# Gathered rows as matmul weights: transposed sums, 32 targets per tile, and a set-up with fewer products

## The chip, the cores and the metric

The kernel runs on one core of a Trainium2 chip. A core has five engines with queues of their own: PE (TensorE, matrix products), DVE (VectorE), ACT (ScalarE), POOL (GpSimd, which here issues the indirect gathers) and SP (SyncE, which issues plain transfers). Sixteen DMA engines move the data. The metric is the time on the device in microseconds; the kernel before takes 1398.12 us, the median of three runs (1397.97 to 1398.96).

## The reference

Everything is float32. For B = 16 batches, N = 1024 nodes and D = 256 features, with `adj` a sparse weighted adjacency that serves as both A_a and A_m:

```python
pre_u  = einsum('bud,dk->buk', h, W1[:d])
pre_v  = einsum('bvd,dk->bvk', h, W1[d:])
hidden = relu(pre_u[:, :, None, :] + pre_v[:, None, :, :] + b1)
S   = sigmoid(einsum('buvk,ko->buvo', hidden, W2)[..., 0] + b2[0])
a_t = einsum('buv,bud->bvd', S * A_a, h)
m_t = einsum('uv,bud->bvd', A_m, h) * h
z   = beta1*h + beta2*(a_t @ Wa + ba) + beta3*(m_t @ Wm + bm)
```

Of the 1024 x 1024 pairs (u, v) 9052 have an edge. The kernels compute the gate only for these.

## The kernel before

**Tiles and loops.** The 1024 targets v are cut into 8 blocks of 128, each block into two windows of 64. The edges of a window are laid out one after another, sorted by target, in five tiles of 128 slots. The 16 batches are worked through in 4 groups of 4. So there are 32 block steps (`k`, group by group), ten tiles each, 320 tiles (`n`).

**Lists (`lists`).** For each block DVE finds up to 24 sources per target (line 173, three rounds of eight maxima), numbers their slots, and builds a 0/1 matrix that says which target owns which slot (`mark`). It goes to DRAM (`who`) and is loaded from there for each window (`load_mark`, line 420). Five matrix products with that matrix as weights (line 211) carry target data to slots. From them come the indices `uidx`, `vidx` and a one-hot row of 64 targets per slot. Then POOL gathers the edge values, ten small indirect transfers per list, all at once (line 237). Four lists (`EARLY`) are made ahead of the tiles, the others beside the first tiles, one step of the generator per tile.

**Rows (`rows`).** For each 128 nodes and each group, PE multiplies the transposed input hT with the two halves of W1 (line 291). The u half goes to a DRAM table, next to a copy of x (a row is 2048 numbers: 1024 of pre_u and 1024 of h). The v half gets b1 from DVE (`keep`, line 280) and stays in `pv`. In the set-up both halves are made for all eight blocks of group 0; those of the next group are made beside the tiles of the present one.

**Halves (`halves`).** For the block to come, `pv` is split in a rounded part and a remainder (lines 310 to 325), so that one pass in the format fp32r over both gives the full value. PE swaps the remainder to the other 64 partitions with a permutation (line 322).

**A tile.** `fetch` (line 411) gathers 128 table rows of 8 KB into one of five buffers. `expand` (line 427) spreads the targets' pre_v over the slots: mark as weights, two products of 512 columns. `gate` adds the two on DVE (line 441), takes ReLU times W2 with a sum (line 445, one instruction per batch), and ACT does the sigmoid (line 448). `left_adj` (line 435) makes one-hot times edge value, and line 450 multiplies it with the gate. `aggregate` (line 458) has these 128 columns, 64 targets without and 64 with the gate, as weights and the gathered h, 256 columns, as moving operand: four products per tile, whose sums of 128 partitions (two kinds of 64 targets) x 256 gather in `acc` over the five tiles.

**Window and block end.** ACT copies `acc` to `ev` (line 465), DVE multiplies the ungated half with h (line 469), PE transposes the whole (line 480) and ACT copies it to `LT` (lines 482, 483). `block_end` multiplies with Wm and Wa (line 498, `LT` as weights), and DVE adds beta1 h and the biases (lines 490, 504).

**Order.** Each engine does its instructions in the order of the program; that order is written by hand in the loop over `n` (a step per tile), and `after(step, f)` puts work off to a later step. At step n: aggregation of tile n-1, the fetch that its buffer allows, gate of tile n, put-off work, window and block ends, a step of the lists, pieces of the halves and rows, and the expansion of tile n+2. POOL's queue holds value gathers and row fetches in the order of issue.

Of the kernel before, what the change touches and what calls it, by code (L numbers as in the profile page):

```python
# [17 lines left out]
def kernel(  # L18
# [36 lines left out]

    nc = tc.nc
# [10 lines left out]
    S = 24  # L67
    RC = 5 + S
# [7 lines left out]
    who = [dram.tile([W, E], FP, name=f"who{w}") for w in range(NT * NW)]  # L76
# [42 lines left out]

    ahead = fixed([P, P], "ahead")  # L120
# [10 lines left out]
    slot, nth, place = upto, upto[:, :S], upto[:, :W]  # L131
# [4 lines left out]
    onehot = const.tile([P, NT * NW, TW, W], mybir.dt.bfloat16, name="onehot")  # L136
# [10 lines left out]
    pvp = main.enter_context(tc.tile_pool(name="pvp", bufs=NT))  # L147
# [13 lines left out]
    def lists(vt):  # L161
# [6 lines left out]
        unread = one.tile([P, N], mybir.dt.bfloat16, name="unread")  # L168
# [12 lines left out]
        nc.vector.scalar_tensor_tensor(R[:, 4:5], late, -float(W), row, ALU.mult, ALU.add)  # L181
# [8 lines left out]
        nc.vector.tensor_scalar(held, first, -1.0, float(E), ALU.mult, ALU.add)  # L190
        nc.vector.tensor_scalar(held, held, 0.0, R[:, 0:1], ALU.max, ALU.min)
        nc.vector.tensor_tensor(R[:, 0:1], R[:, 0:1], first, ALU.add)
        nc.vector.tensor_tensor(rest[:, vt:vt + 1], count, held, ALU.subtract)
        early = wk.tile([P, E], FP, name="early", bufs=1)
        nc.vector.tensor_scalar(early, slot, R[:, 0:1], None, ALU.is_lt)
# [3 lines left out]
        mark = big.tile([P, E], FP, name="made", bufs=2)  # L199
        nc.vector.scalar_tensor_tensor(mark, slot, first, early, ALU.is_ge, ALU.mult)  # L200
# [4 lines left out]
        RR = wk.tile([P, NW, RC], FP, name="RR", bufs=2)  # L205
        for w, mine in enumerate((soon, late)):
            nc.vector.tensor_scalar(RR[:, w, :], R, mine, None, ALU.mult)
            nc.sync.dma_start(who[vt * NW + w], mark[w * W:(w + 1) * W])
        pe = aside(vt)
        for j in range(TW):  # L210
# [6 lines left out]
                       pe[:, :M * RC].rearrange("p (j w r) -> p w j r", w=NW, r=RC))  # L217
        s_of = wk.tile([P, M], FP, name="s_of", bufs=2)
# [12 lines left out]
        yield  # L231
        nc.vector.tensor_tensor(onehot[:, sl].rearrange("p w j v -> p (w j) v"),
                                place.unsqueeze(1).to_broadcast([P, M, W]),
                                L[:, :, 4:5].to_broadcast([P, M, W]), ALU.is_equal)
        for i in range(vt * NW, (vt + 1) * NW):
            for j in range(TW):
                nc.gpsimd.indirect_dma_start(  # L237
                    out=val[:, i, j:j + 1], out_offset=None, in_=adj_flat,
                    in_offset=bass.IndirectOffsetOnAxis(ap=vidx[:, i, j:j + 1], axis=0),
                    bounds_check=N * N - 1, oob_is_err=False)  # L240
# [16 lines left out]
    pv, hTs = {}, {}  # L257

    def load_hT(k):
        g, nt = divmod(k, NT)  # L260
        if g < NG:
            hTs[k] = big.tile([P, GB, DC, P], FP, name="hT")
            nc.sync.dma_start(hTs[k].rearrange("p b c n -> p (b c) n"),
                              xT_rows[:, g * GB * DC:(g + 1) * GB * DC, nt * P:(nt + 1) * P])

    def rows(k):

        g, nt = divmod(k, NT)
        step = yield
        load_hT(k + 1)  # L270
        nc.scalar.dma_start(table[g][nt * P:(nt + 1) * P, GD:].rearrange("n (b d) -> n b d", b=GB),
                            x_rows[nt * P:(nt + 1) * P, g * GB:(g + 1) * GB, :])
        hT = hTs.pop(k)
        tab = big.tile([P, GD], FP, name="tab")

        def keep(c, p):
            if c.start == 0:
                pv[k] = pvp.tile([P, GD], FP, name="pv")
            m = (c.stop - c.start) // D
            nc.vector.tensor_tensor(pv[k][:, c].rearrange("p (b d) -> p b d", b=m),  # L280
                                    p.rearrange("p (b d) -> p b d", b=m),
                                    b1_b.unsqueeze(1).to_broadcast([P, m, D]), ALU.add)
        for wt in (w_u, w_v):
            for h in range(2):
                c = slice(2 * h * D, (2 * h + 2) * D)
                if wt is w_v and g == 0 and h == 0:
                    both = psa.tile([P, GD], FP, name="acc")
                p = both[:, c] if wt is w_v and g == 0 else small("p")
                for bb in range(2):
                    for i in range(DC):  # L290
                        nc.tensor.matmul(p[:, bb * D:(bb + 1) * D], hT[:, 2 * h + bb, i, :], wt[:, i, :],  # L291
                                         start=(i == 0), stop=(i == DC - 1))
                if wt is w_u:
                    nc.scalar.copy(tab[:, c], p)  # L294
                    if h == 1:
                        after(step + 1, lambda: nc.sync.dma_start(table[g][nt * P:(nt + 1) * P, :GD], tab))
                elif g:
                    after(step + 1, lambda c=c, p=p: keep(c, p))
                elif h == 1:
                    after(step + 1, lambda both=both: keep(slice(0, GD), both))  # L300
                if h == 0 or wt is w_u:
                    step = yield
# [218 lines left out]
    for n in range(NF):  # L521
        fetch(n)
# [160 lines left out]
```

## Time and profile before

| what | us |
|---|---|
| median of three runs | 1398.12 |
| profiled execution | 1396.24 |
| its span | 1394.4 |
| PE busy / PE weight loads busy | 1268.1 / 1076.6 |
| DVE busy | 1189.4 |
| ACT busy | 901.2 |
| POOL busy | 453.9 |

The busy times overlap. A PE share close to one means that matmul records follow one another without a gap; what a record costs is read from the distance between starts. The DMA queues moved 411.38 MB, 296.70 of them the gathers of POOL's queue.

### The profile page before, as it was taken

What the parts mean: (1) busy time and instruction counts of PE and PEld (TensorE: products, weight loads), DVE (VectorE), ACT (ScalarE), POOL (GpSimd) and SP (SyncE); (2) the same over time, 40 slices, a digit from 0 to 9 for tenths busy, and PEclk for the clock granted to TensorE, in tenths of its full rate; (3) what the DMA queues carried; (4) which work ended last, traced back from release to release, by engine and by line L of the source; (5) the groups of instructions that cost most, each with busy time, mean ns of one, the idle gap of its engine ahead of it and who ended that gap; (6) DMA issues with size and microseconds to landing.
All of it is one profiled execution on the core that took longest, in us unless ns stands there. A gap on an engine that the chain in (4) does not pass through costs nothing.

```text
span 1394.4 us, 20649 instructions
## 1 busy us (share of the span) xinstructions
PE 1268.1 (91%) x5920; PEld 1076.6 (77%) x5920; DVE 1189.4 (85%) x3424; ACT 901.2 (65%) x2554; POOL 453.9 (33%) x411
## 2 busy tenths in 40 slices
PE   6854888878999999999999999999999989999997
PEld 5743766667888888888888888888888777777775
DVE  8736898897888998888888998888888999999995
ACT  3113555555767777777776776767767777777763
POOL 2564245244322332222222322222222333333330
PEclk9976999989999999999999999999999999999999
DMA  6757856956999999999999899999998998999992
GB/s 190 225 170 280 274 197 229 328 182 229 339 354 313 312 363 334 310 323 346 334 331 314 308 349 333 315 313 331 331 343 302 322 322 307 310 310 317 314 320 76
DMA packets 152250, 411.38 MB, mean 295 GB/s; under 512 B 18128, under 2 KB 101584, under 8 KB 115920
## 3 DMA queue, kind: packets, MB, share of 16 engines
q0 software_dynamic: 48640, 296.70, 60.3%
q1 hardware_dynamic: 74112, 73.93, 16.2%
q10 hardware_dynamic: 29376, 39.33, 9.6%
q8 instruction: 50, 0.82, 0.2%
q14 instruction: 72, 0.59, 0.1%
HBM read 412.66 MB, written 52.95 MB: 334 GB/s over the span
## 4 chain that ended last, share of the span: by engine, by line
issue 32%; DVE 27%; DMA 13%; PE 12%; POOL 11%; ACT 3%; POOLq 1%; SPq 0%; DVEq 0%; ACTq 0%
POOL fetched L411 11%; DMA fetched<-table,uidx 10%; DVE t L445 10%; DVE t L441 9%; PE acc L458 4%; PE misc L291 3%; PE misc L498 2%; ACT left L450 1%; DVE ev L469 1%; DMA key<-in_adjT_dram 1%; DVE R L173 1%; DVE h_blk L490 1%; DMA val<-in_adjT_dram,vidx 1%; PE pc L427 1%; DMA hT<-in_xT_dram 1%
## 5 line engine op out<-in xcount | busy, mean ns | idle before, releaser
L458 PE MATMUL acc<-fetched,left 128*128 128x256 f32 x2560 | 618.0, 385 | 38.8 <-ACT ev L465 19.5
L411 POOL DMA_INDIRECT fetched<-table,uidx x320 | 350.6, 1096 | 839.6 <-PE acc L458 703.9
L458 PEld LDWEIGHTS acc<-fetched,left 128*128 128x128 f32 x2560 | 486.4, 192 | 134.5 <-ACT left L450 33.4
L445 DVE SCALAR_TENSOR_TENSOR t<-t,w_b 128x256 f32<-128x256 f32 x1280 | 470.0, 422 | 21.5
L441 DVE TENSOR_TENSOR t<-fetched,pc 128x1024 f32<-128x1024 f32 x320 | 388.7, 1215 | 96.3 <-DMA fetched<-table,uidx 62.2
L450 ACT ACTIVATE left<-left,gt 128x64 f32<-128x64 f32 x1280 | 340.9, 337 | 10.4
L427 PE MATMUL pc<-X,mark 128*128 128x512 f32 x640 | 244.1, 463 | 31.1 <-DVE t L441 28.0
L448 ACT ACTIVATE gt<-sc,b_b 128x4 f32<-128x4 f32 x320 | 95.8, 299 | 269.8 <-DVE t L445 268.1
L435 ACT ACTIVATE left<-onehot,val 128x256 f32<-128x256 bf16 x320 | 157.8, 493 | 2.1 <-DMA hT<-in_xT_dram 2.1
L427 PEld LDWEIGHTS pc<-X,mark 128*128 128x128 f32 x640 | 118.2, 192 | 47.4 <-DVE t L441 29.2
L498 PE MATMUL misc<-w_m,LT 128*128 128x256 f32 x512 | 135.1, 387 | 6.6 <-ACT LT L483 2.9
L291 PE MATMUL misc<-w_u,hT 128*128 128x256 f32 x512 | 125.1, 390 | 11.7 <-DMA hT<-in_xT_dram 8.7
L498 PE MATMUL misc<-w_a,LT 128*128 128x256 f32 x512 | 131.9, 380 | 0.0
L291 PEld LDWEIGHTS misc<-w_u,hT 128*128 128x128 f32 x512 | 98.2, 195 | 26.5 <-issue 8.7
L498 PEld LDWEIGHTS misc<-w_m,LT 128*128 128x128 f32 x512 | 96.2, 192 | 27.1 <-DVE h_blk L504 8.4
L237 POOL DMA_INDIRECT val<-in_adjT_dram,vidx x80 | 92.6, 1158 | 67.9 <-DVE eq L221 36.3
L294 ACT COPY tab<-misc 128x512 f32<-128x512 f32 x64 | 37.4, 584 | 116.8 <-PE misc L291 104.3
L498 PEld LDWEIGHTS misc<-w_a,LT 128*128 128x128 f32 x512 | 97.6, 191 | 13.3
L445 DVE DVE_READ_ACCUMULATOR t<-t,w_b 128x1 f32 x1280 | 104.2, 81 | 0.0
L325 ACT CAST X<-misc 64x512 fp32r<-64x512 f32 x128 | 74.2, 580 | 34.6 <-PE misc L322 32.7
L291 PE MATMUL misc<-w_v,hT 128*128 128x256 f32 x384 | 91.2, 380 | 2.0 <-ACT LT L483 1.7
L469 DVE TENSOR_TENSOR ev<-ev,h_blk 64x1024 f32<-64x1024 f32 x64 | 78.0, 1219 | 10.6 <-ACT ev L465 9.6
(90 smaller groups left out, 915.2 us busy)
## 6 DMA issues: line engine op xcount, KB each, us to landing
mark<-who ACTq DMA_DIRECT2D x128, 160.0 KB, 7.7
hT<-in_xT_dram SPq DMA_DIRECT2D x32, 512.0 KB, 10.3
table<-in_x_dram ACTq DMA_DIRECT2D x32, 512.0 KB, 8.8
table<-tab SPq DMA_DIRECT2D x32, 512.0 KB, 7.9
h_blk<-in_x_dram SPq DMA_DIRECT2D x32, 512.0 KB, 15.8
out_dram<-h_blk SPq DMA_DIRECT2D x32, 512.0 KB, 5.3
fetched<-table,uidx POOLq DMA_INDIRECT x320, 8.7
key<-in_adjT_dram SPq DMA_DIRECT2D x8, 512.0 KB, 8.1
```

The source lines that it names most:

```text
L237: nc.gpsimd.indirect_dma_start(out=val[:, i, j:j + 1], out_offset=None, in_=adj_flat, in_offset=bass.IndirectOffsetOnAxis(ap=vidx[:, i, j: ...
L291: nc.tensor.matmul(p[:, bb * D:(bb + 1) * D], hT[:, 2 * h + bb, i, :], wt[:, i, :], start=(i == 0), stop=(i == DC - 1))
L411: nc.gpsimd.indirect_dma_start(out=fetched[n % NF], out_offset=None, in_=table[g], in_offset=bass.IndirectOffsetOnAxis(ap=uidx[:, vt * NW ...
L427: nc.tensor.matmul(pcs[n][:, c], marks[n // TW][:, j * P:(j + 1) * P], cuts[k][:, w, c], start=True, stop=True)
L435: nc.scalar.activation(lefts[n][:, :, w, :], onehot[:, i, j, :].unsqueeze(1).to_broadcast([P, GB, W]), AF.Copy, scale=val[:, i, j:j + 1])
L441: nc.vector.tensor_tensor(t, fetched[n % NF][:, :GD].rearrange("p (b d) -> p b d", b=GB), pcs.pop(n).rearrange("p (b d) -> p b d", b=GB), ...
L445: nc.vector.scalar_tensor_tensor(t[:, b, :], t[:, b, :], 0.0, w2_b, ALU.max, ALU.mult, accum_out=sc[:, b:b + 1])
L448: nc.scalar.activation(gt, sc, AF.Sigmoid, bias=b2_b)
L450: nc.scalar.activation(lefts[n][:, b, 1 - w, :], lefts[n][:, b, w, :], AF.Copy, scale=gt[:, b:b + 1])
L458: nc.tensor.matmul(accs[n // TW][:, b, :], left[:, b].rearrange("p k v -> p (k v)"), f[:, GD + b * D:GD + (b + 1) * D], start=(j == 0 and ...
L469: nc.vector.tensor_tensor(ev[m0:m0 + W], ev[m0:m0 + W], hbs[k][m0:m0 + W], ALU.mult)
L498: nc.tensor.matmul(pz[:, bb * D:(bb + 1) * D], LTs[k][:, b * DC + c, i, :], wt[:, c, :], start=(i == 0 and c == 0), stop=(i == 1 and c == ...
```

## The change

- **Aggregation.** Per tile and batch there are now two products instead of one: a gathered block of 128 slots x 128 features is the weights, and 64 columns (32 targets without and with the gate) move. The sums come out with features on partitions and targets on columns. Tile j of a window holds only targets from `LO[j]` to `LO[j]` + 31, with `LO` = 0, 6, 20, 32, 32; an edge outside goes to the loop at the end of the kernel that handles what is left. The one-hot rows, `left` and the scaling by the gate have 32 columns instead of 64.
- **Window end.** Two ACT copies bring the sums to `LT`, ahead of the next gate; DVE multiplies with hT. Transposes, `ev` and the four copies are gone.
- **hT** stays in ten buffers for a group. Its load and the copy of x to the table are issued at one step of a block.
- **w_v and b1.** The v half is made in `halves`, one block ahead, for every block; b1 is added by a matrix product with an all-ones matrix and fp32r parts of b1 in two partitions (`spread`, `add_row`). So the set-up makes the u half only.
- **Block end.** The biases come in the same way, and h times beta1 is added in the instruction that reads the product.
- **Marks.** The 0/1 matrix is kept as bytes in SBUF for all windows (`whose`), written there by four SBUF transfers per list, and ACT casts it for each window.
- **Order.** `EARLY` is 3 instead of 4. Value gathers go to a list (`wanted`) and are issued two at a time next to the row fetches. One more step lies between the copy of `L` and its readers.

```diff
-    onehot = const.tile([P, NT * NW, TW, W], mybir.dt.bfloat16, name="onehot")
+    onehot = const.tile([P, NT * NW, TW, V], mybir.dt.bfloat16, name="onehot")
+    whose = const.tile([P, NT * NW, E], mybir.dt.uint8, name="whose")
...
+        few = wk.tile([P, E], mybir.dt.uint8, name="few", bufs=2)
+        nc.scalar.copy(few, mark)
         for w, mine in enumerate((soon, late)):
             nc.vector.tensor_scalar(RR[:, w, :], R, mine, None, ALU.mult)
-            nc.sync.dma_start(who[vt * NW + w], mark[w * W:(w + 1) * W])
+            for h in range(2):
+                nc.sync.dma_start(whose[h * W:(h + 1) * W, vt * NW + w, :], few[w * W:(w + 1) * W])
...
+        wanted.extend((i, j) for i in range(vt * NW, (vt + 1) * NW) for j in range(TW))
+    def fetch_val(n):
+        for i, j in wanted[:n]:
+            nc.gpsimd.indirect_dma_start(
+                out=val[:, i, j:j + 1], out_offset=None, in_=adj_flat,
+                in_offset=bass.IndirectOffsetOnAxis(ap=vidx[:, i, j:j + 1], axis=0),
+                bounds_check=N * N - 1, oob_is_err=False)
+        del wanted[:n]
...
+    def add_row(p, parts):
+        nc.tensor.matmul(p, unit, parts.unsqueeze(1).to_broadcast([P, 2, D]),
+                         start=True, stop=False, skip_group_check=True)
...
     def halves(k):
-        top = one.tile([P, GD], FR, name="top")
-        nc.scalar.copy(top, pv[k])
-        yield
         X = cuts[k] = big.tile([P, NW, GD], FR, name="X")
         low = one.tile([P, GD], FR, name="low")
...
+        for h in range(2):
+            step = yield
+            c = slice(2 * h * D, (2 * h + 2) * D)
+            p = small("p")
+            add_row(p, b1_p)
+            half_product(p, hTs[k], w_v, h, True)
+            nc.scalar.copy(X[:, 0, c], p)
+            after(step + 1, lambda c=c, p=p: nc.vector.tensor_tensor(
+                low[:, c], p, X[:, 0, c].bitcast(FP), ALU.subtract))
...
     def load_mark(q):
         marks[q] = big.tile([P, E], FR, name="mark")
-        src = who[q % (NT * NW)]
-        for h in range(2):
-            nc.scalar.dma_start(marks[q][h * W:(h + 1) * W].bitcast(FP), src)
+        nc.scalar.copy(marks[q], whose[:, q % (NT * NW), :])
...
         for b in range(GB):
-            nc.tensor.matmul(accs[n // TW][:, b, :], left[:, b].rearrange("p k v -> p (k v)"),
-                             f[:, GD + b * D:GD + (b + 1) * D],
-                             start=(j == 0 and b % 2 == 0), stop=(j == TW - 1), skip_group_check=True)
+            for c in range(DC):
+                d = GD + b * D + c * P
+                nc.tensor.matmul(acc[:, b, c, :, LO[j]:LO[j] + V], f[:, d:d + P], left[:, 0:b + 2:b + 1, :],
+                                 start=(j == 0 and b % 2 == 0 and c == 0), stop=(j == TW - 1),
+                                 skip_group_check=True)
...
     def window_end(q, step):
...
+        for h in range(2):
+            i = slice(h * GB * DC // 2, (h + 1) * GB * DC // 2)
+            nc.scalar.copy(LT[:, i, :, v], acc[:, h * GB // 2:(h + 1) * GB // 2].rearrange("p b c k v -> p (b c) k v"))
         def times_h():
+            nc.vector.tensor_tensor(LT[:, :, 0, v], LT[:, :, 0, v],
+                                    hTs[k].rearrange("p b c n -> p (b c) n")[:, :, v], ALU.mult)
...
         if 1 <= n <= total:
             aggregate(n - 1)
+            fetch_val(2)
             if n - 1 + NF < total:
                 fetch(n - 1 + NF)
+            if n % TW == 0:
+                window_end(n // TW - 1, n)
         if n < total:
             gate(n)
```

290 lines of the change are left out of this document (146 added, 144 removed).

## The prediction

> **What bounds the kernel now.** I first cut the span by the add that opens each tile's gate (line 441): the set-up up to tile 0, tiles 0 to 49, 50 to 239, 240 to 309, and the last ten with the tail; one row more takes tiles 10 to 39. Columns of the first view: stretch and its us, then busy us (and instructions) of PE, PE weight loads, DVE, ACT and POOL, granted PE clock, DMA share, GB/s. The second counts the adds.
>
> ```profile
> 0.00:117.70 117.70, 71.69 (x318) 59.87 (x318) 70.00 (x162) 23.32 (x38) 59.94 (x55) 0.87 0.62 186
> 117.70:367.00 249.30, 206.98 (x907) 168.57 (x908) 217.35 (x625) 141.06 (x397) 101.32 (x89) 0.94 0.75 260
> 159.70:320.90 161.20, 133.19 (x591) 107.61 (x592) 140.10 (x398) 88.10 (x247) 70.17 (x60) 0.96 0.72 247
> 367.00:1094.00 727.00, 722.30 (x3447) 625.95 (x3446) 641.45 (x1866) 525.58 (x1502) 203.25 (x191) 1.00 0.95 327
> 1094.00:1338.80 244.80, 224.39 (x1052) 187.07 (x1051) 225.48 (x673) 186.01 (x541) 81.24 (x70) 1.00 0.92 315
> 1338.80:1394.40 55.60, 42.75 (x201) 35.13 (x199) 35.12 (x101) 25.24 (x82) 8.13 (x7) 0.97 0.51 180
> ```
> ```profile
> 117.70:367.00 249.30, 60.73 (x50) 0.94 0.75 260
> 159.70:320.90 161.20, 36.43 (x30) 0.96 0.72 247
> 367.00:1094.00 727.00, 230.80 (x190) 1.00 0.95 327
> 1094.00:1338.80 244.80, 85.00 (x70) 1.00 0.92 315
> ```
>
> So there are five stages with different limits. **A**, the set-up, 117.7 us. **B**, 50 tiles while the remaining edge lists are built, 4.99 us each; DVE is the busiest (87%). **C**, 190 tiles at 3.83 us, 38.3 us per block of ten: PE is busy 722 of 727 us, and nothing else can set the pace. **D**, 70 tiles at 3.50 us, without row products: DVE and PE both 92%. **E**, 55.6 us.
>
> Then the timeline around the end of A:
>
> ```profile
> 81.97 0.33 SPq L296 DMA_DIRECT2D table<-tab  x1
> ...
> 84.89 1.12 POOL L237 DMA_INDIRECT val<-in_adjT_dram,vidx  x1 [7.81 <-DVE s_of L219]
> ...
> 88.22 1.22 DVE L280 TENSOR_TENSOR pv<-acc,b_b 128x1024 f32<-128x1024 f32 x1
> ...
> 110.29 0.99 POOL L237 DMA_INDIRECT val<-in_adjT_dram,vidx  x1 [0.30 <-issue]
> 111.58 1.00 POOL L411 DMA_INDIRECT fetched<-table,uidx  x1 [0.30 <-issue]
> ...
> 117.77 1.22 DVE L441 TENSOR_TENSOR t<-fetched,pc 128x1024 f32<-128x1024 f32 x1 [28.33 <-DMA fetched<-table,uidx]
> ```
> ```profile
> table<-tab SPq DMA_DIRECT2D x32, 512.0 KB, 7.9
> ```
>
> DVE is done at 89.4 and the table at 82.0 + 7.9 = 89.9, but POOL first works off twenty edge-value gathers, 1.3 us apart, from 84.9 to 111.3. Row fetches stand behind them, and DVE waits 28 us.
>
> **The change, stage by stage.**
>
> *A.* The gathers are now issued two at a time, ahead of row fetches, so POOL's queue no longer holds the first fetch; the table is late next, and with it DVE. DVE's busy 70.0 us lose the eight bias adds (1.22 each, 9.8) and one list of four. A list costs 140.10/30 - 641.45/190 = 1.29 us per tile over ten tiles, 12.9 us. Some 34 constant instructions come in, mostly tiny ones of the kind below, the rest up to a bias copy's size: 6 us, an estimate.
>
> ```profile
> L198 DVE TENSOR_SCALAR held<-held 128x1 f32<-128x1 f32 x8 | 1.2, 154 | 0.3
> ```
>
> 70.0 - 9.8 - 12.9 + 6 = 53 us busy. At the present 78% (70.0/89.4) DVE ends at 68. The last two row pieces, their write (7.9) and the way from first fetch to first gate (117.77 - 111.58 = 6.2) follow partly behind it; I put the fetch at 72 and the first gate at 78. Bounds: DVE without any wait, 53 + 1 + 6.2 = 60; three lists at the 20 us apiece that they now occupy, 8 + 62 + 7 for the start and the constants, then 7.9 and 6.2, 91. PE's work here falls by w_v's half of the products, so it is no bound. **-40** (-58 to -27).
>
> *B.* Five lists instead of four run here, with the same DVE. Its other work:
>
> ```profile
> L469 DVE TENSOR_TENSOR ev<-ev,h_blk 64x1024 f32<-64x1024 f32 x64 | 78.0, 1219 | 10.6 <-ACT ev L465 9.6
> ...
> L504 DVE TENSOR_TENSOR h_blk<-misc,h_blk 128x512 f32<-128x512 f32 x64 | 44.0, 687 | 12.8 <-PE misc L498 12.7
> L490 DVE SCALAR_TENSOR_TENSOR h_blk<-h_blk,be,bias 128x1024 f32<-128x1024 f32 x32 | 41.0, 1280 | 0.0
> L314 DVE TENSOR_TENSOR low<-pv,top 128x1024 fp32r<-128x1024 f32 x32 | 39.0, 1219 | 0.0
> ...
> L280 DVE TENSOR_TENSOR pv<-misc,b_b 128x512 f32<-128x512 f32 x48 | 33.1, 690 | 16.2 <-PE misc L291 15.8
> ```
>
> Per block the bias adds go (2 x 0.69), and so does the scaled bias (1.28). The product with h becomes two of 512 columns at 0.69 instead of two at 1.22 (-1.06); the remainder `low` becomes two of 0.69 for 1.22 (+0.16). That is -3.56 per block, -18 over five blocks, +12.9 for the fifth list: 212 us busy of the present 217.35. Of the 32 us idle, this wait makes up most (17.1 in 150 to 367 us):
>
> ```profile
> DVE s_of L219 <- ACT L L216: 17.1, 4, 5.3
> ```
>
> The added step between the copy of L and its reader lets a gate run in between; I count 13 of the 17 as gained: 212 + 19 = 231. **-18** (-27, idle of 10; -5, idle unchanged).
>
> *C.* PE alone counts.
>
> ```profile
> 701.59 1.03 PE L498 MATMUL misc<-w_a,LT 128*128 128x256 f32 x4
> 702.26 0.81 PE L427 MATMUL pc<-X,mark 128*128 128x512 f32 x2
> 702.91 1.89 PE L458 MATMUL acc<-fetched,left 128*128 128x256 f32 x8
> 704.64 0.59 PE L291 MATMUL misc<-w_u,hT 128*128 128x256 f32 x2
> ```
> ```profile
> 36.34 1.32 PE L211 MATMUL pc<-RR,made 128*128 128x58 f32 x10
> 37.50 1.95 PE L291 MATMUL misc<-w_u,hT 128*128 128x256 f32 x8
> 39.29 1.22 PE L211 MATMUL pc<-RR,made 128*128 128x58 f32 x10
> 40.34 0.87 PE L291 MATMUL misc<-w_u,hT 128*128 128x256 f32 x3
> ```
> ```profile
> 708.55 1.04 PE L480 MATMUL misc<-ident,ev 128*128 128x128 f32 x8
> ```
>
> Starts, not durations, give the price, as matmuls overlap. A written fp32 product is two records. Today's aggregation is eight records per tile, (704.64 - 702.91)/8 = 216 ns apart. The new one has twice the products, each with a gathered 128 x 128 block as weights and 64 moving columns: sixteen records. Nearest is line 211 with 58 columns: ten records take 1.16 and 1.05 us, 116 and 105 ns apart, mean 110.5. Four times fewer columns only halve the price, so something other than the stream, which I take for the weight load, sets it. Per tile 16 x 0.1105 = 1.77 us for 1.73; per block +0.4. Line 480's sixteen transposes per block go, the spacing being about 109 ns (1.04 us less one record of 0.275, over 7): -1.74. Four bias rows of 512 columns are added; the pair of line 427 lies between four 216 ns records from 701.59 (to 702.45) and 702.91, so one costs 0.23: +0.93. Sum -0.41 per block, over 19 blocks **-8**. With 105 ns it is -25. For the dear end I read the weight loads of such a ten, 1.30 us less one of 0.19 over 9, 123 ns: +30. A row at 58 columns is so near to 64 that I keep its mean.
>
> *D.* Group 3's w_v products, formerly made ahead, now come here. PE without stalls: aggregation 17.3, line 427 4.6, block end 6.9, transposes 1.7, swap 0.5, 31 us per block (224.39/7 = 32.1 busy). After: 31 - 0.41 + 16 x 0.216 = 34.1, against 35.0 per block today; DVE falls to 32.2 - 2.2 = 30. I take 34.6, PE-bound: **-3** (-9 to +13).
>
> *E.* The tail loses the transposes and their copies:
>
> ```profile
> 1376.22 1.01 ACT L465 COPY ev<-acc 128x1024 f32<-128x1024 f32 x1 [1.37 <-PE acc L458]
> ...
> 1379.94 1.13 PE L498 MATMUL misc<-w_m,LT 128*128 128x256 f32 x4 [0.30 <-ACT LT L483]
> ```
>
> From the copy to the first product is 3.7 us; two ACT copies (1.17) and one DVE product (0.69) make 1.9. With a little DVE work saved, **-3**.
>
> At nothing I cost what PE's 99% in C hides: a mark matrix is now cast by ACT instead of loaded by DMA, about 0.7 us per window by the 0.584 us of 512 columns below, while ACT is busy 525.58 of 727 and loses four transposition copies per window; its cover gone, it is 0.14 us a tile. The hT loads and table copies move to one fixed step of a block, on the same SP and ACT queues, with the row product six steps (23 us) behind them, and what a table copy finds late would be the first fetches of the next group, six steps on. On SP a list's byte writes wait for one more ACT cast, and behind them stand hT loads and table writes; in B these have those same 23 us, in A they are inside the bounds above.
>
> **Sum.** -40 - 18 - 8 - 3 - 3 = -72: span 1394.4 to 1322.4. The profiled execution took 1396.24 (1.84 more), the median 1398.12 (another 1.9): **1326**.
>
> **Rivals.**
>
> 1. *The set-up gives half.* The table's last row, not POOL, may already be nearly as late: hT loads, table copies and writes share the DMA engines (0.62 busy in A) and the list writes hold SP. First gate at 97: 1326 + 19 = **1345**. For: PE and DVE wait for each other in A; against: the table stood at 90 with one list more.
>
> 2. *The window copies delay the gates.* ACT now copies the sums before the gate's sigmoid, so at each window end it sits waiting for the aggregation's last product with the sigmoid queued behind; PE's next aggregation waits for that sigmoid's weights.
>
> ```profile
> L448 ACT ACTIVATE gt<-sc,b_b 128x4 f32<-128x4 f32 x320 | 95.8, 299 | 269.8 <-DVE t L445 268.1
> ...
> L450 ACT ACTIVATE left<-left,gt 128x64 f32<-128x64 f32 x1280 | 340.9, 337 | 10.4
> ...
> L294 ACT COPY tab<-misc 128x512 f32<-128x512 f32 x64 | 37.4, 584 | 116.8 <-PE misc L291 104.3
> ```
>
> The way is 2 x 0.584 + 0.30 + 0.34 = 1.8 us. Covering it on PE are eight records of a block's end or of w_v (1.73) and the next expansion (0.46), 2.2 us. Were the cover gone, 52 window ends in C and D cost 94 us: 1326 + 94 = **1420, slower**; it decides from 72/52 = 1.4 us each. Against: 0.4 us are to spare.
>
> 3. *Weight loads do not hide.* The mean load row says 192 ns:
>
> ```profile
> L458 PEld LDWEIGHTS acc<-fetched,left 128*128 128x128 f32 x2560 | 486.4, 192 | 134.5 <-ACT left L450 33.4
> ```
>
> At 192 ns per record a tile takes 3.07 us, 1.30 more than forecast: +351 over the 270 tiles from C on, and in B PE's 207 + 65 us would pass the 231 by 41: about **1720**. If only the stream's share (64/256 of 216 = 54 ns) is added to the 110, 164 ns, it is +0.85 per tile, 230 and 19 in B: **1575**. The gain is eaten at 72/270/16 = 17 ns more, 127 ns. Against: 512 columns in 230 ns and 256 in 216 leave no room for a bare load, and line 211's records hold their load already.
> The Trainium skill, "TensorE: Matmul & The Clock Gate", part 3, The mechanism, says that weight loads overlap running matmuls only where the row group differs; all here use all rows, so by it the time would be the 1575. The trace disagrees: the rows just named show loads hidden at full rows.
>
> 4. *PE gets cheaper than that*: 100 ns and below by way of the long run of equal records. Then C falls towards DVE's 641.45/19 - 3.56 = 30 us, but DMA (0.95 busy, less 5% for the marks) holds it near 36: 19 x 1.9 less, **1290**.
>
> 5. *A target's edges miss their 32-wide tile* and the slow loop at the end runs. Counting the reference's adjacency, the fullest window has 607 edges and no edge misses its tile; I leave it no chance.
>
> **Chances.** Forecast 0.66, rival 1 0.12, rival 2 0.08 (three parts in four past the point), rival 3 0.07, rival 4 0.07. What a measurement can tell from no change is 0.2%, 3 us. Faster: 0.66 + 0.12 + 0.07 and a little of rival 2, 0.85; same 0.02; slower 0.13. The forecast's own range lets A, B, C and D be off by half of their bounds, all to one side: 25 less, 40 more, 1301 to 1366. The range takes in rivals 1 and 4 and the near side of 2: **1288 to 1372**.
>
> **What would show it.** The first gate's add at 78 us, with no run of value gathers ahead of the first fetch; 50 tiles in 231 us; aggregations of sixteen records near 110 ns apart, 1.77 us a tile, with PE over 98% busy in C at 37.9 us per block; D at 34.6 with PE the busiest. I am wrong if those records lie 127 ns apart or more, if PE idles at window ends for ACT's copies, or if the first gate comes after 100 us.

## The result and the profile after

The changed kernel takes **1355.89 us** (median of four runs, 1353.14 to 1358.41) against 1398.05 for the kernel before on the same chip: a ratio of **0.9704**, interval 0.9677 to 0.9731. Forecast were 1326 us, range 1288 to 1372. Of 72 us only 42 came. One run of `once` (below), 1386.93 us, was in a slower state of the chip, and its time there is that of the other three.

The profiled execution took 1355.8 us, its span is 1353.9. Here is the changed kernel cut by the add that opens each gate (line 494 now), with the columns of the prediction's first view:

```profile
0.00:90.00 90.00, 50.25 (x197) 39.37 (x197) 53.34 (x158) 23.64 (x39) 17.69 (x18) 0.86 0.75 227
90.00:339.70 249.70, 224.45 (x1244) 199.65 (x1244) 216.81 (x659) 123.56 (x388) 128.27 (x120) 0.84 0.75 250
339.70:1056.40 716.70, 716.70 (x4763) 664.58 (x4763) 582.76 (x1827) 434.18 (x1430) 206.62 (x197) 1.00 0.89 313
1056.40:1296.10 239.70, 239.70 (x1640) 223.14 (x1640) 212.12 (x672) 153.53 (x512) 75.14 (x71) 1.00 0.85 304
1296.10:1353.90 57.80, 46.59 (x259) 40.90 (x258) 31.34 (x97) 18.45 (x68) 7.37 (x7) 0.81 0.45 160
```

| stage | before | forecast | after | change forecast / measured |
|---|---|---|---|---|
| A, set-up to first gate | 117.7 | 78 | 90.0 | -40 / -27.7 |
| B, tiles 0 to 49 | 249.3 | 231 | 249.7 | -18 / +0.4 |
| C, tiles 50 to 239 | 727.0 | 719 | 716.7 | -8 / -10.3 |
| D, tiles 240 to 309 | 244.8 | 242 | 239.7 | -3 / -5.1 |
| E, last ten and tail | 55.6 | 52.6 | 57.8 | -3 / +2.2 |

The stages that PE bounds came slightly better than forecast. A gave two thirds, B nothing, and E went the wrong way. In B DVE is as busy as before (216.81 of 217.35) and the granted PE clock has fallen from 0.94 to 0.84, in E from 0.97 to 0.81.

The end of A, from the timeline of the changed kernel (start, duration, engine, instruction, in brackets the idle time before it and its releaser):

```profile
67.82 1.32 PE L251 MATMUL pc<-RR,made 128*128 128x58 f32 x10 [1.16 <-DVE RR L246]
68.98 3.68 PE L319 MATMUL misc<-w_u,hT 128*128 128x256 f32 x16
...
70.37 3.26 SPq L336 DMA_DIRECT2D table<-tab  x2
...
71.85 0.49 DVE L272 TENSOR_TENSOR onehot<-place,L 128x320 bf16<-128x320 f32 x1
...
82.31 1.00 POOL L467 DMA_INDIRECT fetched<-table,uidx  x1 [34.24 <-DMA table<-in_x_dram]
...
90.04 1.22 DVE L494 TENSOR_TENSOR t<-fetched,pc 128x1024 f32<-128x1024 f32 x1 [17.70 <-DMA fetched<-table,uidx]
```

No run of value gathers stands ahead of the first fetch any more; POOL has been idle for 34 us when it comes, and the releaser is a transfer to the table. The last row pieces stand in PE's queue behind the third list's product, which PE waits 1.16 us for; the later of the two row writes starts at 70.37 + 3.26 - 0.33 = 73.3. It lands 8.0 us later, at 81.3, and the fetch comes 1.0 us behind that. (The releaser's row names a copy of x. This group's last copy was issued at 69.2 already; the one issued at 72.7, which lands in the same moment as the row write, fills the next group's table, which this fetch doesn't read.) DVE's lists end at 72.3. From there to the fetch it takes 10 us, and to the gate another 7.7.

What DVE waits for in B of the changed kernel (us in total, times, longest; 17.7 of the first row is the wait that ends A):

```profile
DVE t L494 <- DMA fetched<-table,uidx: 18.0, 2, 17.7
DVE t L494 <- PE pc L481: 9.8, 4, 4.7
DVE key L206 <- DMA key<-in_adjT_dram: 9.2, 3, 4.0
DVE low L352 <- ACT X L351: 4.4, 3, 2.2
...
DVE s_of L260 <- ACT L L256: 0.3, 1, 0.3
```

And the same view of the kernel before:

```profile
DVE s_of L219 <- ACT L L216: 17.1, 4, 5.3
DVE key L169 <- DMA key<-in_adjT_dram: 1.8, 1, 1.8
...
DVE t L441 <- PE pc L427: 1.3, 1, 1.3
```

The wait that the prediction meant to see shrink went from 17.1 to 0.3 us. Three others took its place: the load of the next list's adjacency rows (`key`, 1.8 to 9.2), the expansions (1.3 to 9.8) and the rounded part of pre_v (`low`, 4.4).

In C, a tile's aggregation and its neighbours in PE's queue:

```profile
702.85 0.81 PE L481 MATMUL pc<-X,mark 128*128 128x512 f32 x2
703.50 1.89 PE L513 MATMUL acc<-left,fetched 128*128 128x64 f32 x16
705.23 1.08 PE L548 MATMUL misc<-w_m,LT 128*128 128x256 f32 x4
```

Sixteen records take 705.23 - 703.50 = 1.73 us, 108 ns each; forecast were 110.5. Three stretches of B show one of two clocks (the ninth column):

```profile
113.20:140.40 27.20, 25.20 (x99) 22.99 (x99) 21.87 (x74) 13.18 (x43) 18.47 (x19) 0.50 0.82 264
140.50:174.50 34.00, 31.15 (x201) 27.74 (x199) 31.51 (x90) 17.05 (x57) 19.02 (x18) 1.00 0.74 242
174.60:191.60 17.00, 16.01 (x58) 14.44 (x59) 13.51 (x50) 7.29 (x21) 2.43 (x3) 0.50 0.82 255
```

At 0.50 PE's records are busy for 25.20 of 27.20 us, 93%, and it gets 99 of them done in 27 us instead of 201 in 34. What stands right before the first fall of the clock in B, and the later part of the stretch behind it:

```profile
109.60:113.00 3.40, 1.57 (x10) 1.00 (x9) 3.25 (x8) 0.00 (x0) 2.79 (x3) 1.00 1.00 285
119.80:136.90 17.10, 17.06 (x70) 16.22 (x71) 14.81 (x58) 8.76 (x28) 12.92 (x14) 0.50 0.76 232
```

PE was busy for 1.57 of the 3.40 us before the fall, mostly because it waited 1.78 us for DVE. The other eight falls in B and E, up to PE's last product, come behind 3.40 us with 1.03 to 2.69 us of PE work. So a fall follows PE's waiting. Once down, the clock stays at 0.50 for 17 us in which PE's records leave no gap.

### The profile page after: what moved, and what is told of

Its sections match the earlier page's. It is cut to its first block, busy times and chain, and to the rows that moved or that the text cites. A ratio compares the mean times of both kernels' runs of the same rounds, so it can differ in the third digit from the quotient of the medians.

```text
span 1353.9 us, 24556 instructions
## 1 busy us (share of the span) xinstructions
PE 1277.7 (94%) x8096; PEld 1167.6 (86%) x8096; DVE 1096.4 (81%) x3413; ACT 753.4 (56%) x2434; POOL 435.1 (32%) x411
## 4 chain that ended last, share of the span: by engine, by line
PE 66%; DVE 12%; issue 8%; DMA 7%; POOL 3%; ACT 2%; SPq 1%; ACTq 0%; POOLq 0%; DVEq 0%
PE acc L513 29%; PE misc L548 13%; PE misc L319 12%; PE pc L481 8%; DVE t L498 4%; DMA fetched<-table,uidx 4%; DVE t L494 3%; POOL fetched L467 2%; PE misc L323 2%; DMA key<-in_adjT_dram 2%; DVE R L210 1%; POOL val L282 1%; PE misc L360 1%; DMA table<-in_x_dram 1%; ACT LT L526 1%
## 5 line engine op out<-in xcount | busy, mean ns | idle before, releaser
L513 PEld LDWEIGHTS acc<-left,fetched 128*128 128x128 f32 x5120 | 637.0, 196 | 50.6 <-ACT left L503 23.8
L513 PE MATMUL acc<-left,fetched 128*128 128x64 f32 x5120 | 625.2, 277 | 15.4 <-ACT left L503 15.4
L467 POOL DMA_INDIRECT fetched<-table,uidx x320 | 339.8, 1062 | 827.2 <-PE acc L513 613.9
L503 ACT ACTIVATE left<-left,gt 128x32 f32<-128x32 f32 x1280 | 306.5, 310 | 10.4
L481 PE MATMUL pc<-X,mark 128*128 128x512 f32 x640 | 251.9, 475 | 19.6 <-DVE t L494 18.1
L526 ACT COPY LT<-acc 128x512 f32<-128x512 f32 x128 | 68.7, 589 | 216.5 <-PE acc L513 216.5
L319 PE MATMUL misc<-w_u,hT 128*128 128x256 f32 x512 | 136.5, 416 | 17.8 <-DMA hT<-in_xT_dram 9.5
L319 PE MATMUL misc<-w_v,hT 128*128 128x256 f32 x512 | 122.7, 383 | 0.0
L548 PEld LDWEIGHTS misc<-w_a,LT 128*128 128x128 f32 x512 | 100.5, 196 | 14.5
L319 PEld LDWEIGHTS misc<-w_v,hT 128*128 128x128 f32 x512 | 99.0, 193 | 13.1
L489 ACT ACTIVATE left<-onehot,val 128x32 f32<-128x32 bf16 x320 | 97.7, 305 | 0.0
## 6 DMA issues: line engine op xcount, KB each, us to landing
h_blk<-in_x_dram SPq DMA_DIRECT2D x32, 512.0 KB, 12.7
```

The lines of the kernel that those rows point to most:

```text
L467: nc.gpsimd.indirect_dma_start(out=fetched[n % NF], out_offset=None, in_=table[g], in_offset=bass.IndirectOffsetOnAxis(ap=uidx[:, vt * NW ...
L481: nc.tensor.matmul(pcs[n][:, c], marks[n // TW][:, j * P:(j + 1) * P], cuts[k][:, w, c], start=True, stop=True)
L489: nc.scalar.activation(lefts[n][:, 0, :], onehot[:, i, j, :], AF.Copy, scale=val[:, i, j:j + 1])
L503: nc.scalar.activation(lefts[n][:, 1 + b, :], lefts[n][:, 0, :], AF.Copy, scale=gt[:, b:b + 1])
L513: nc.tensor.matmul(acc[:, b, c, :, LO[j]:LO[j] + V], f[:, d:d + P], left[:, 0:b + 2:b + 1, :], start=(j == 0 and b % 2 == 0 and c == 0), s ...
L526: nc.scalar.copy(LT[:, i, :, v], acc[:, h * GB // 2:(h + 1) * GB // 2].rearrange("p b c k v -> p (b c) k v"))
```

## The experiments

The theory after the result had three parts: the late table holds A; the waits for `key` and PE's lower clock take back the gain of B; the clock takes E. The rivals: in B one of the two alone, or nothing but DVE's own work; and in C that the 64 columns have a price. Stages are those of the table above, each from the profiled execution of the kernel.

**v64: 128 columns instead of 64.** All 64 targets of a window stay in each tile, so the moving operand is twice as wide and the products as many.

```diff
-    V = 32
-    LO = [0, 6, 20, 32, 32]
+    V = 64
+    LO = [0, 0, 0, 0, 0]
```
The one-hot rows compare with `upto[:, :V]` in place of `place`, are bytes instead of bf16, and `RR` has one buffer instead of two, for space.

> Every tile again takes all 64 targets of its window, so each aggregation product moves 128 columns instead of 64 with the same weights. Clock theory (stage B and the tail lost time because 64-column products leave the array idle half of the time and the clock is granted at half speed): granted clock in B, tiles 0 to 49, from 0.84 to 0.92 or more, B from 250 us to 240, the tail stage E from 58 to 55; C (tiles 50 to 239) and D stay at 717 and 240 us within 5, because the spacing of the records, 110 ns, is set by the weight load. Feeding theory (B lost its gain to late keys and the fifth list, the low clock only follows from PE waiting): clock and B unchanged. Third view, columns set the price: spacing 140 ns or more and C longer by over 90 us. Total by the clock theory 1343, by the feeding theory 1356, by the third over 1440.

Measured: **1342.78 us**, ratio 0.9587 (0.9561 to 0.9613): faster than with 64 columns. From v64's windows (B, C, E, then the first fall of the clock in its B) and its PE timeline:

```profile
90.52:334.15 243.63, 211.41 (x1243) 187.65 (x1244) 218.49 (x659) 130.16 (x388) 129.15 (x120) 0.90 0.77 256
334.15:1050.24 716.09, 716.09 (x4759) 663.46 (x4757) 583.00 (x1827) 459.32 (x1427) 207.96 (x197) 1.00 0.89 314
...
1291.68:1343.77 52.09, 40.47 (x268) 36.18 (x266) 31.25 (x97) 20.69 (x72) 7.75 (x7) 0.95 0.50 183
...
110.00:113.40 3.40, 1.68 (x11) 1.08 (x9) 3.25 (x6) 0.00 (x0) 2.79 (x3) 1.00 0.94 280
113.40:120.20 6.80, 4.67 (x19) 3.92 (x18) 6.73 (x18) 2.99 (x10) 5.28 (x6) 0.50 0.82 297
```
```profile
701.89 1.95 PE L509 MATMUL acc<-left,fetched 128*128 128x128 f32 x16
703.60 0.48 PE L356 MATMUL misc<-low,swap 128*128 128x512 f32 x1
```

Sixteen records take 703.60 - 701.89 = 1.71 us at 128 columns, 107 ns each, and C is 716.1 against 716.7. The second 64 columns are free: something that every record has, not its columns, sets its price. E falls by 5.7 us, with the clock at 0.95 instead of 0.81. B falls by 6.1, which two profiles of one kernel can differ by as well (the run "again", below). The clock falls at the same place as before and behind the same kind of gap, but is back at 1.00 after 6.8 us, the longest time in v64's B, instead of 27.3: the columns show in how long it stays down.

**warm: more work for PE in B.** Four bias rows that the expansion then overwrites go ahead of each of the first 50 expansions, 200 records of 0.23 us, 46 us of PE.

```diff
+        if n < 50:
+            for h in range(4):
+                add_row(pcs[n][:, (h % 2) * 2 * D:(h % 2 + 1) * 2 * D], b1_p)
```

> In the first 50 tiles four throw-away one-pass products of 512 columns (0.23 us each, 46 us of PE work in all) are put ahead of each expansion, into the same accumulator, which the expansion then overwrites. Clock theory: granted clock in B 0.95 or more, and B no longer than 250 us, rather 240, in spite of the added work. Feeding theory: the clock may rise, but B gets longer, 255 to 270 us, since PE's 224 busy us of 250 get 46 more. C, D and E unchanged within 4 us.

Measured: 1346.75 us, ratio 0.9623 (0.9602 to 0.9644). B of warm, and two of its waits:

```profile
90.08:331.32 241.24, 235.05 (x1436) 211.22 (x1436) 217.47 (x660) 123.89 (x388) 128.73 (x120) 0.97 0.77 258
```
```profile
DVE t L497 <- PE pc L484: 9.6, 7, 3.6
...
DVE key L206 <- DMA key<-in_adjT_dram: 0.3, 1, 0.3
```

With 46 us more work on PE, B is 8.5 us shorter and the clock is 0.97. But the waits for expansions, which a faster clock should shorten, stay at 9.6 (the added rows stand right ahead of the expansions), and the waits for `key` are gone, for a reason that the run doesn't show. So it doesn't separate the two causes.

**keyahead: the adjacency rows of the next list are loaded a list earlier.**

```diff
-        key = big.tile([P, N], FP, name="key", bufs=2)
-        nc.sync.dma_start(key, adjT[vt * P:(vt + 1) * P, :])
+        if vt not in keys:
+            load_key(vt)
...
+        key = keys.pop(vt)
...
+        if EARLY <= vt < NT - 1:
+            load_key(vt + 1)
```

> The key rows of the next list are loaded half a list (some 20 us) before they are used, for the lists built beside the tiles. Feeding theory: DVE's waits for the key in B go from 9.2 us to under 1, B from 250 to 241 us, and the clock in B rises a little with it; total 1347. Clock theory: the waits go, but B loses only part of them, 245 us or more, and the clock stays under 0.88; total 1352.

Measured: 1343.76 us, ratio 0.9618 (0.9584 to 0.9652). B of keyahead, and its DVE waits:

```profile
90.32:326.71 236.39, 214.69 (x1246) 192.48 (x1246) 216.62 (x658) 123.55 (x388) 128.87 (x119) 0.87 0.78 262
```
```profile
DVE t L503 <- PE pc L490: 8.5, 4, 4.7
DVE low L361 <- ACT X L360: 4.5, 3, 2.2
DVE s_of L269 <- ACT L L265: 0.3, 1, 0.3
```

No row for `key` is left, the others are as they were, and B is 13.3 us shorter, at a clock of 0.87. That is more than the 9.2 us of waits; the B of a single profile is known to about 10 us only (the run "again", below). On the same chip rowsfirst, with the changed kernel's tiles, has 247.3, 10.9 more than keyahead, and the medians of the runs, 1355.89 and 1343.76, lie 12.1 apart.

**v64key: both together**, the edits of v64 and keyahead.

> 64 targets per tile and keys half a list ahead, set-up as in the changed kernel. If the granted clock and the keys are separate causes in B, their gains add: 6 and 13 us, B 231 within 3, total 1330. If the keys' waits were in good part what brought the clock down, or the clock's waits fall on the same places, B stays at 236, as with the keys alone, and only E's 6 us come on top: total 1336.

Measured: 1345.51 us, ratio 0.9606 (0.9571 to 0.964), 9 us above the second branch; the changed kernel itself is as much slower on this chip (again, 1364.44). B is 240.6 us at a clock of 0.92, with no wait for `key` of any weight, so the gains don't add in B. Over all eleven kernels with the change, B takes 236.4 to 241.2 in the five that wait less than 0.5 us for `key` (keyahead, warm, v64key, best, best2; clock 0.87 to 0.97) and 243.6 to 260.0 in the six that wait 5.4 to 9.2 us (clock 0.82 to 0.90). So the waits part the two groups. Within the first the clock orders nothing: the shortest B has the lowest clock, 0.87. Within the second the longest B has the lowest clock, but longer other waits too. What the clock costs in B by itself stays open. In E both kernels with 128 columns agree: 52.1 us, clock 0.95 and 0.98.

**gath: the kernel before, with the value gathers put off** and issued two at a time, and nothing else of the change.

```diff
-        for i in range(vt * NW, (vt + 1) * NW):
-            for j in range(TW):
-                nc.gpsimd.indirect_dma_start(...)
+        wanted.extend((i, j) for i in range(vt * NW, (vt + 1) * NW) for j in range(TW))
...
+            fetch_val(2)
```

> The kernel before, with one part of the change alone: value gathers go to a list and are issued two at a time beside the row fetches. Theory that POOL's queue held the first fetch there: first fetch from 111.6 to 90 to 92 us (the table stands at 89.9), first gate from 117.8 to 97 to 99, B about as before, total 20 us less, ratio 0.985. Rival, the gathers only filled time in which something else was late: first gate not before 110, ratio 0.995 or more.

Measured: 1386.09 us, ratio 0.9899 (0.9876 to 0.9922), 14 us less than the 1400.29 of the kernel before beside it, where 20 were expected. From gath's timeline:

```profile
88.25 1.27 POOL L416 DMA_INDIRECT fetched<-table,uidx  x1 [38.52 <-DMA mark<-who]
...
96.53 1.22 DVE L446 TENSOR_TENSOR t<-fetched,pc 128x1024 f32<-128x1024 f32 x1 [6.74 <-DMA fetched<-table,uidx]
```

The first fetch moves from 111.6 to 88.3 and the first gate from 117.8 to 96.5: POOL's queue was what held A of the kernel before, worth 21 us there. B then takes 255.5 instead of 249.3, so a third of it is lost again. That is within what two profiles of one kernel differ by in B, and its cause isn't shown.

**once: the changed kernel with a list's ten gathers issued at once**, as before the change.

```diff
         wanted.extend((i, j) for i in range(vt * NW, (vt + 1) * NW) for j in range(TW))
+        fetch_val(10)
```

> The changed kernel with the gathers of a list issued at once again, ten in a row. If the shorter set-up comes from the gathers: first fetch at 100 us or later, total 15 us or more above the changed kernel. If the shorter set-up comes from having one list and the v products less in it: twenty gathers fit between 45 and 72 us and ten more end at 85, first fetch at 85 to 87 instead of 82.3, B up to 10 us longer since fetches stand behind bursts, total 3 to 13 us above the changed kernel's 1356.

Measured: 1366.65 us (1364.1 to 1374.5), ratio 0.9776 (0.9732 to 0.982). From once's timeline:

```profile
74.43 0.58 ACT L336 COPY tab<-misc 128x512 f32<-128x512 f32 x1 [9.52 <-remote]
...
78.57 0.99 POOL L283 DMA_INDIRECT val<-in_adjT_dram,vidx  x1 [6.31 <-DVE vidx L271]
...
91.57 1.00 POOL L468 DMA_INDIRECT fetched<-table,uidx  x1 [0.30 <-issue]
```

The third list's ten gathers run from 78.6 and the first fetch comes behind them, 9.3 us later than in the changed kernel and between the two branches; the first gate is 7.4 later (97.4) and B 7.7 longer (257.4). Not all of the 9.3 us is the gathers': ACT's copy of a row piece sat idle 9.5 us for a reason that the profile doesn't name, the third list was 6 us late with it, and the last row write was issued at 79.3 instead of 73.3. So this run doesn't give the price of the ten gathers alone. D and E came out 4.3 shorter, so the spans differ by 10.9 (1364.8).

**rowsfirst: the rows paced as if fewer list steps had to run beside them**, so that the table's pieces come earlier.

```diff
-        for _ in range((m + 1) * 10 * EARLY // OP - m * 10 * EARLY // OP):
+        for _ in range((m + 1) * 20 // OP - m * 20 // OP):
```

> In the set-up the third list is built behind the row products instead of between them (20 list steps beside the 16 row pieces instead of 30, the rest behind). Theory that the table is what the first fetch waits for, since PE holds its last two row pieces behind the third list's products: last table write 10 us or more earlier, first fetch from 82.3 to 62 to 70 us, first gate from 90 to 72 to 78, then with DVE's lists as the bound; total 1342. Rival, the DMA engines are the bound of the set-up: first fetch not before 78, first gate not before 85, total 1352 or more.

Measured: 1354.53 us, ratio 0.967 (0.9639 to 0.9701): a miss. From rowsfirst's timeline:

```profile
72.03 2.39 SPq L248 DMA_DIRECT2D whose<-few  x4
74.46 0.58 SPq L336 DMA_DIRECT2D table<-tab  x1
...
82.76 0.99 POOL L467 DMA_INDIRECT fetched<-table,uidx  x1 [25.56 <-DMA table<-in_x_dram]
```

PE made the rows earlier, but in SP's queue the last table write stands behind the third list's byte writes, which wait for that list. It goes out at 74.46, lands 7.3 us later, and the fetch comes at 82.76, again 1.0 us behind the landing. This group's last copy of x had been issued at 55.4 already, so of this group's transfers it is the row write that holds the fetch. The edit moved the work and not its transfer.

**rows2: the same, and the last table write ahead of these byte writes**, with the block weights' loads moved to SP and the first copy for the next group behind the first fetches.

```diff
+    do(-10)
+    late_loads()
...
-    do(-10)
...
-    copy_h(NT)
...
+    copy_h(NT)
```

> As rowsfirst, but the last table write is issued ahead of the third list's byte writes on SP, the late weight loads go from ACT's queue to SP's, behind that write, and the copy of x for group 1 stands behind the first fetches. In rowsfirst the last write was issued at 74.5 us only, behind those byte writes, so it told nothing on the table. Theory, the table is what the first fetch waits for: first fetch at 62 to 72 us, and then DVE's third list is late, first gate 76 to 82, total 8 to 14 us under the changed kernel's. Rival, the DMA engines bound the set-up: first fetch not before 78, first gate not before 85.

Measured: **1339.28 us**, ratio 0.9551 (0.9525 to 0.9577). From rows2's timeline:

```profile
56.43 0.32 SPq L336 DMA_DIRECT2D table<-tab  x1
...
61.66 1.00 POOL L470 DMA_INDIRECT fetched<-table,uidx  x1 [8.08 <-DMA bias<-in_bm_dram]
...
73.75 0.48 DVE L272 TENSOR_TENSOR onehot<-place,L 128x320 bf16<-128x320 f32 x1
74.15 1.21 DVE L497 TENSOR_TENSOR t<-fetched,pc 128x1024 f32<-128x1024 f32 x1
```

The write goes out 17 us earlier, the fetch comes 20.6 us earlier, and the first gate follows DVE's last list instruction directly, at 74.15. With the table early, A is 4 us under the forecast's 78, and the DMA engines weren't its bound: the rival wanted the first fetch not before 78. The edit moves the late loads and a copy of x as well, so the 17 us aren't shown to be the write's alone.

**best: v64, keyahead and rows2 in one.**

> 64 targets per tile, keys loaded half a list ahead and the set-up of rows2 together. If clock and keys are separate causes, they add: B 250 to 231 (keys 13, clock 6), C and D 717 and 241 unchanged, E 58 to 52, first gate 90 to 79; total 1322, ratio 0.944. If they are one cause, B stays at 236 or more and the total is 1328 or more.

Measured: **1324.11 us**, ratio 0.9452 (0.9433 to 0.947). The stages are 75.8, 237.0, 717.3, 241.4 and 52.0; against the changed kernel A gives 14.2, B 12.7 and E 5.8 of the 30.5 us of span. B is that of the second branch, 236 or more: keys and columns don't add there.

**best2: best, with the biases back on DVE from block 5 on**, where PE has no gap and DVE has.

```diff
-            add_row(p, b1_p)
-            half_product(p, hTs[k], w_v, h, True)
+            half_product(p, hTs[k], w_v, h, False)
...
-                    add_row(pz, bias_p)
+                    if by_pe:
+                        add_row(pz, bias_p)
+                    elif h == 0:
+                        after(step + 1, lambda: nc.vector.scalar_tensor_tensor(
+                            hb, hb, be1, bias.unsqueeze(1).to_broadcast([P, GB, D]), ALU.mult, ALU.add))
```
b1 goes into the table's u half instead, added by PE for the first rows and by DVE for the others.

> As best, and from block 5 on the biases are again added by DVE: b1 to the u half where it is written to the table (in the set-up and for the first five row blocks by a product), the scaled bias once per block. It takes four one-pass products of 512 columns per block off PE, 0.93 us, and gives DVE 2.7 us in C and 1.3 in D. Theory that PE alone sets the pace of C and D: C from 717 to 699, D from 241 to 235, total 1324 to 1300, ratio 0.929. Rival, DVE's chain or the DMA engines are nearly as tight: C at 708 or more, total 1312 or more.

Measured: **1307.85 us** (1303.18 to 1310.89), ratio **0.933** (0.9307 to 0.9354), the fastest of all. C and D of best2:

```profile
315.06:1017.87 702.81, 700.69 (x4683) 650.88 (x4682) 620.44 (x1884) 442.21 (x1392) 210.89 (x198) 1.00 0.90 321
1017.87:1252.90 235.03, 235.03 (x1612) 216.88 (x1611) 217.69 (x679) 162.49 (x512) 75.28 (x71) 1.00 0.85 308
```

C falls by 14.5 us against best and D by 6.3, where 18 and 6 were expected; the total is 8 us above the expected 1300. DVE takes 37.6 us more in C (582.80 to 620.44) and doesn't set the pace: PE is still busy 700.69 of 702.81.

**again: the changed kernel itself once more, beside these on another chip.**

> The changed kernel itself once more, as the base beside the two others and to see how far a stage differs between two profiled executions: A 90 us, B 250 within 3, C 717 within 1, D 240 within 2, E 58 within 1; total 1356 within 3.

Measured: 1364.44 us, ratio 0.9727 (0.9706 to 0.9748). The stages are 91.3, 260.0, 716.2, 240.5 and 58.0. Only B differs, by 10 us, and one wait for `low` makes it up (again, DVE's waits in B, and PE's timeline at that wait):

```profile
DVE low L352 <- ACT X L351: 12.5, 1, 12.5
```
```profile
105.16 0.38 PE L319 MATMUL misc<-w_u,hT 128*128 128x256 f32 x1 [0.36 <-issue]
106.57 0.38 PE L319 MATMUL misc<-w_u,hT 128*128 128x256 f32 x1 [1.04 <-issue]
109.41 0.59 PE L319 MATMUL misc<-w_u,hT 128*128 128x256 f32 x1 [2.46 <-issue]
110.82 1.31 PE L319 MATMUL misc<-w_u,hT 128*128 128x256 f32 x2 [0.82 <-issue]
```

PE does its row products one by one here, with gaps for which no releaser shows, and all that follows in its queue is late. Such spells, with starts 1.41 to 1.46 us apart, stand in B of once, v64key and best2 too, and in none of the four profiles from the chip of keyahead (v64, warm, keyahead, rowsfirst). So a B of one profile is known to about 10 us, and differences of 13 us are told by their waits, not by the sum alone.

## Why the prediction was right, and where it was wrong

The total lies inside the range but 30 us above the forecast. A, B and E missed by 12, 19 and 5 us, all to the same side; C and D came out 2 us better each. The range holds this because it was drawn wide enough for rival 1, which foresaw a miss in A; those in B and E were not foreseen.

**A (-40, measured -27.7).** The bound was read rightly: gath shows POOL's queue alone to be worth 21 us. The busy time was right, 53.34 us against 53. What failed is the term "DVE ends at 68 ... I put the fetch at 72 and the first gate at 78". DVE's lists ended at 72.3 (4.3 later); the fetch came 10 us behind them instead of 4; the first gate 7.7 behind the fetch instead of 6. Together 12 us. The 4 us took the last row pieces and their write to run mostly beside DVE's lists. In the changed kernel they stand behind the third list's product on PE, and a write of 7.9 us can't hide behind a list that is all but over; rows2 moved the write (and other transfers with it) and brought the fetch to 61.7 and the gate to 74.15. Rival 1 ("the table's last row, not POOL, may already be nearly as late") named the mechanism and put the gate at 97; 90.0 lies between. Its reason "the list writes hold SP" is what rowsfirst ran into.

**B (-18, measured +0.4).** Two steps failed. DVE's work was put at 212 and measured 216.81: in C it fell by (641.45 - 582.76)/19 = 3.09 us per block instead of 3.56, which is 2.4 over B's five blocks; that leaves 216.81 - 217.35 + 5 x 3.09 = 14.9 instead of 12.9 for the fifth list and whatever else is new in B. The larger one is "I count 13 of the 17 as gained". The wait itself vanished as said, but the prediction did not ask what is late next. DVE, free 17 us sooner, ran into the next list's adjacency rows, whose load is issued only when the list begins. keyahead gave 13.3 us back, to 236.4; DVE's idle time is then 236.4 - 216.6 = 19.8, the forecast's 19, and the rest of the way to 231 is DVE's 5 us. The waits for expansions (9.8) stand in keyahead too (8.5) and are not what separates 249.7 from 236.4.

**C (-8, measured -10.3).** Right in mechanism and size: records at 108 ns for 110.5, PE busy in the whole stage, 716.70/19 = 37.7 us per block for 37.9. That the floor is the weight load, as the prediction took it, no run separates from other work that every record has.

**D (-3, measured -5.1).** Right: 239.7/7 = 34.2 us per block for 34.6, PE-bound, and DVE at 212.12/7 = 30.3 for 30.

**E (-3, measured +2.2).** The step that the forecast priced came as said: from the copy at 1334.8 to the first product at 1336.6 it takes 1.9 us. The forecast's 52.6 is also what the kernels with 128 columns show (52.0 to 53.2). The sum had no term for the granted clock, which went from 0.97 to 0.81 here. v64 alone changes the columns and has 0.95 and 52.1, so the clock is worth 5.7 us. Kernels with 64 columns bear it out: five at a clock of 0.81 take 57.8 to 58.4 us, warm at 0.85 56.5 and once at 0.91 54.9. In E one chain is followed from engine to engine and PE's own speed lies on it: eight records of a block's end on it take 3.41 us at the low clock (from 1307.4) and 1.78 at the full one (from 1313.2).

**The rivals.** Window copies (2): no; PE is busy for all of C with two copies at every window end, the cover held. Weight loads that do not hide (3): no, by 108 ns; v64 at 107 ns with twice the columns leaves nothing of a price per column either. The page "TensorE: Matmul & The Clock Gate", part 3, The mechanism, of the Trainium skill, by which loads overlap only where row groups differ, is not borne out by these records, which all use the full rows. The same section of the Trainium skill also lets a load be pulled ahead when it goes to a background weight buffer; whether these loads do, no run here shows. Cheaper records (4): no, 108.

**The clock.** The same page of the Trainium skill, part 1, The HAM clock gate, gives two ratios for the clock, 4/8 and 8/8. This agrees with the stretches of B at 0.50 and 1.00. That page of the Trainium skill puts the lower one down to an idle window of some 3.4 us and the higher one to a busy one. The falls agree in part: PE waited before each of the nine, but for 0.7 to 2.4 of the last 3.4 us and not for all of them. The return doesn't agree: in 17.10 us with PE's records busy for 17.06 the clock stayed at 0.50. That few columns keep it down is borne out by v64: after a like fall it is low for 6.8 us instead of 27.3, and the mean goes from 0.84 to 0.90 in B and from 0.81 to 0.95 in E, with the same number of products on PE. Columns aren't all of it, since warm and once have 64 and reach 0.85 and 0.91 in E. What the gate counts no run here shows.

## What to carry to other kernels

When a wait or a queue's block is taken away, follow the freed engine to its next input and ask when that input's transfer is issued, and behind what in its queue: here both stages that fell short (the table's write in A, the adjacency rows in B) were in the main repaired by an earlier issue, with the same work. Cutting the columns of a matmul whose record has a floor saves nothing and can lower the granted clock; where a stage is bound by PE, take whole records off it, as the biases of best2 did. A moved step should be followed to its last transfer: rowsfirst did the work earlier and won nothing, since the write kept its place in the queue.

## What the runs showed of the hardware that was not expected

- A float32 record with full weights takes 108 ns at 64 and 107 ns at 128 moving columns, and 216 at 256. The floor thus ends between 128 and 256 columns.
- With 64 columns the granted clock was 0.50 for stretches of 17 and 27 us with PE's records busy over 90%. It fell only behind stretches in which PE had waited (1.03 to 2.69 us of work in 3.40), and in C, with PE never idle, it stayed at 1.00 with the same columns. With 128 columns such a fall lasted 6.8 us instead of 27.3.
- PE can draw its instructions with gaps of 0.4 to 2.5 us that no semaphore explains (again, 105 to 112 us), and one such spell cost 12.5 us on DVE. In the first profile of the same kernel the longest wait for `low` is 2.2 us. The cause is open.
